# An attention and state-space kernel: another lead for the projection, another split of the products with C, and statistics that end later

## The chip, the cores and the metric

The kernel runs on one core of a Trainium2 chip. The metric is the device time of one execution in microseconds (us), from the first instruction to the last. In what follows PE is TensorE (the matmuls), PEld its weight loads, DVE is VectorE, ACT is ScalarE, POOL is GpSimd, and SP is SyncE, which here only issues DMAs. Each of these takes its instructions strictly in the order of the program, and an instruction that waits for a semaphore holds all that stand behind it on its engine.

## The reference, cut to what matters

The input is two images of 256 x 256 positions with 128 channels. Layer 0 is an attention along one image axis, added to its input. Layer 1, the part that matters here, is a state-space block, again added to its input:

```python
g = group_norm(x)                         # 32 groups of 4 channels, over a whole image
xi, z = split(g @ in_proj_w.T)            # 256 inner channels each
xi = silu(depthwise_conv3x3(xi) + conv_b)
dts, Bs, Cs = split(x_proj_w @ xi)        # 8, 16 and 16 rows
delta = softplus(dt_w @ dts + dt_b)
# for each of 256 channels and 16 states, along all 65536 positions of an image:
h[t] = exp(delta[t] * A) * h[t - 1] + (delta[t] * xi[t]) * B[t]
y[t] = sum over states of h[t] * C[t] + D * xi[t]
y = layer_norm(y) * silu(z)
x = x + y @ out_proj_w.T
```

## The kernel before, in words

**Stages.** After the weights are prepared, the statistics of the first image are taken, and the attention of both images runs (L289 to L568). It writes its result x1 to DRAM, and gathers the statistics of x1 on the side. `group_stats` (L204) turns them into a scale `rs` and a shift `sh` for each channel: 32 aggregations on DVE, a matmul with a matrix of 1/128 that averages over partitions, six small operations on DVE, two more matmuls, a power on GpSimd and a last operation on DVE. This happens once for each image and layer; the last of the four ends just ahead of the scan stage.

**Strips, units, slots.** The scan stage works on strips of 4 image rows (T = 1024 positions), 64 for each image, 128 in all. A strip has NU = 32 units: two halves `h` of the channels, in each four groups `m` of states, in each four quarters `q` of 32 channels. A unit is 128 partitions (32 channels x 4 states) x 1024 positions. The order of the stage is written out by hand in the loop at L1051: slot t is the turn of unit t, and the emitted order is the order on PE, ACT, DVE and GpSimd. Below, a slot of the strip is t modulo 32.

In slot t, in this order: `fetch(t + 6)` issues the loads for a later unit; on odd t `drive(t + 3)` (L960) multiplies `du` by B for the pair of units t + 3 and t + 4 on GpSimd, in one instruction of 128 x 2048; `products(t - 2)` (L994) multiplies both units of a *pooled* pair by C on GpSimd; `decay(t + 1)` (L952) is the exponential on ACT, which goes to one of two tiles `da` in PSUM; `scan(t)` (L973) is the recurrence on DVE, 128 x 1024; `product(t)` (L985) multiplies by C on DVE, if the unit is not pooled; `y_out` (L1034) copies the finished y of half the channels out of PSUM on ACT, once every 16 slots; then come pieces of other work that are due in this slot; then `start_up` and `add_up` (L1007, L1017), matmuls that start y with D x and sum products over states; last `remember(t)` (L980), which keeps the last state of the unit on ACT.

A pooled unit's scan writes into `hb`, in SBUF, which GpSimd can read; the others write over `da`. Before, the pairs that begin at units 6, 14, 22, 26 and 30 are pooled, so DVE has 22 of the 32 products of a strip. I number pairs by 0 to 15: drive 13 works for units 26 and 27. The three buffers of `hb` hold a pair each, the three of `du_r` two quarters each.

**Other work in the slots.** `project(k)` (L621) makes what strip k needs, placed by `base`: normalise and transpose x1, 4 times 9 convolution matmuls, the gate z, B, C and delta; three big functions on ACT of 128 x 2048, each between two loads of function tables (`silu_z` at base + 28, `silu_xs` at base + 36, `softplus` at base + 52); and two products `times` on GpSimd (base + 55 and 56). The results are stored to DRAM tiles (`xs_d`, `sz_d`, `bc_d`, `delta_d`, `du_d`) and read back, spread over the partitions, by `fetch`: `bb` and `cc` (B and C of four units), `delta_r` and `du_r` (a quarter of 32 channels). All pieces of `project` that need a PSUM bank take turns in one bank. `finish(k)` (L805) does the layer norm, the gate and the output projection of strip k, a row every 8 slots.

`base` is `k * NU - 72` (L625): the projection of strip k starts 72 slots ahead of the strip's first scan.

**The DMA queue.** SP is not ordered by hand. The framework puts its DMAs in the order in which it estimates that they can be issued; each waits in that order for the engine that made its data or that frees its buffer. In the program of before, the store `sz_d` of strip k + 1 stands in this queue between the loads `du_r` of quarters 1 and 2 of strip k's first half, seven places ahead of the load of quarter 3.

Of the kernel before, what the change touches and what calls it, by code (L numbers as in the profile page):

```python
# [8 lines left out]
F32 = mybir.dt.float32  # L9
AF = mybir.ActivationFunctionType  # L10
ALU = mybir.AluOpType
# [4 lines left out]
P = 128  # L16
# [5 lines left out]
def attn_then_ssm_kernel(  # L22
# [46 lines left out]
    def column(name, src):  # L69

        t = const.tile([P, 1], F32, name=name)
        nc.sync.dma_start(out=t, in_=src.rearrange("(p o) -> p o", o=1))
        return t

# [5 lines left out]

    ident = const.tile([P, P], F32, name="ident")
    make_identity(nc, ident)
    ones_mean = const0.tile([P, P], F32, name="ones_mean")
    nc.vector.memset(ones_mean, 1.0 / P)
# [15 lines left out]
    bq_c = column("bq_c", bq)  # L100
    bv1_c = column("bv1_c", bv1)
# [99 lines left out]
    nc.vector.tensor_tensor(centre[:, P : 2 * P], centre[:, P : 2 * P], ident, ALU.add)  # L201


    def group_stats(stats, pool, psum, name, tag="mm"):  # L204
# [5 lines left out]
        gm_ps = psum.tile([P, G], F32, name="gm_ps", tag=tag)  # L210
        nc.tensor.matmul(gm_ps, ones_mean, mv[:, :, 0], start=True, stop=True)
        gm = pool.tile([P, G], F32, name="gm")
        nc.vector.tensor_copy(gm, gm_ps)
        dev = pool.tile([P, G], F32, name="dev")
        nc.vector.tensor_tensor(dev, mv[:, :, 0], gm, ALU.subtract)
        dev2 = pool.tile([P, G], F32, name="dev2")
        nc.vector.tensor_tensor(dev2, dev, dev, ALU.mult)
        pv = pool.tile([P, G], F32, name="pv")
        nc.vector.tensor_tensor(pv, dev2, mv[:, :, 1], ALU.add)
        ex = pool.tile([P, 2, G, CG], F32, name="ex")  # L220
        nc.vector.tensor_copy(ex[:, 0], gm.unsqueeze(2).to_broadcast([P, G, CG]))
        nc.vector.tensor_copy(ex[:, 1], pv.unsqueeze(2).to_broadcast([P, G, CG]))
        cs_ps = psum.tile([P, 2], F32, name="cs_ps", tag=tag)
        for i in range(2):
            nc.tensor.matmul(
                cs_ps[:, i : i + 1],
                ex[:, i].rearrange("p g c -> p (g c)"),
                ones_mean[:, 0:1],
                start=True,
                stop=True,  # L230
            )
        cs = pool.tile([P, 2], F32, name="cs")
        nc.vector.tensor_copy(cs, cs_ps)
        ve = pool.tile([P, 1], F32, name="ve")
        nc.vector.tensor_scalar(ve, cs[:, 1:2], GN_EPS, None, ALU.add)
        rs = const.tile([P, 1], F32, name=f"rs_{name}")
        nc.gpsimd.tensor_tensor(rs, ve, neg_half[:, 0:1], ALU.pow)
        sh = const.tile([P, 1], F32, name=f"sh_{name}")
        nc.vector.tensor_scalar(sh, cs[:, 0:1], rs, -1.0, ALU.mult, ALU.mult)
        return rs, sh  # L240

    gn0 = {}
    TT = 32
# [31 lines left out]
    NL = LG // LQ  # L275
    NA = W // LQ
    gn1 = {}
    with ExitStack() as actx:
        ap1 = actx.enter_context(tc.tile_pool(name="at1", bufs=1))
        ap = actx.enter_context(tc.tile_pool(name="at", bufs=2))  # L280
# [49 lines left out]
        def project(n, tag, name, w):  # L330
            o = calls[n]
            o[name + "_ps"] = bank(tag, f"{name}_ps", [P, TB])
            nc.tensor.matmul(o[name + "_ps"], w, o["xnc"], start=True, stop=True)
# [150 lines left out]
            nc.vector.bn_stats(stats1[b][:, gr, i, :], x1g[:, :, :, gr * CG : (gr + 1) * CG])  # L484

        def gather(to, b, stats, layer):
            to[b] = group_stats(stats, ap1, ps, f"{layer}_{b}", "t0")

        held = {}

# [96 lines left out]
    NU = NCG * NSG  # L587
    NM = NQ * NSG

    POOLED = (6, 14, 22, 26, 30)  # L590
    s1 = ctx.enter_context(tc.tile_pool(name="s1", bufs=1))
    s2 = ctx.enter_context(tc.tile_pool(name="s2", bufs=2))
    s3 = ctx.enter_context(tc.tile_pool(name="s3", bufs=3))
# [23 lines left out]
    def exp_and_ln():  # L617

        nc.scalar.preload_act_table_set("natural_log_exp_and_others")

    def project(k):  # L621

        b, s = steps[k]
        rs, sh = gn1[b]
        base = k * NU - 72  # L625
        n = min(R, H - 1 - R * s)
        v = given[k] = {}
        o = {}

        def load():  # L630

# [20 lines left out]
                nc.gpsimd.memset(xn[:, 2 + n, 1 : W + 1], 0.0)  # L652

        def turn(src, r, m):
            t_ps = o["t"] = ps_p.tile([P, RB, W], F32, name="t_ps", tag="p")
# [14 lines left out]

        def conv(h, i, taps):
            if taps[0] == 0:
                o["u"] = ps_p.tile([P, RB, W], F32, name="u_ps", tag="p")
# [24 lines left out]
            nc.sync.dma_start(out=v["xs"].rearrange("h p t -> p h t"), in_=o["xs"])  # L698

        def gate(h, i):  # L700
            o["z"] = ps_p.tile([P, RB, W], F32, name="z_ps", tag="p")
# [19 lines left out]
            nc.sync.dma_start(out=v["sz"].rearrange("h p t -> p h t"), in_=o["sz"])  # L721

        def states(i):
            o["xd_ps"] = ps_p.tile([64, TB], F32, name="xd_ps", tag="p")
# [15 lines left out]
            nc.sync.dma_start(out=v["bc"][:, cols], in_=o["xd"][32:64, cols])  # L740

        def size(h, i):
            o["dt"] = ps_p.tile([P, TB], F32, name="dt_ps", tag="p")
# [168 lines left out]
    def unit(t):  # L912

        k, i = divmod(t, NU)
        h, i = divmod(i, NM)
        m, q = divmod(i, NQ)
        return k, h, m, q
# [29 lines left out]
                )  # L947

    def pooled(t):
        return t % NU - t % 2 in POOLED  # L950

    def decay(t):  # L952
        k, h, m, q = unit(t)
# [31 lines left out]
    def product(t):  # L985
        k, h, m, q = unit(t)
        u = units[t]
        if t % 2 == 0:
            yc = s4.tile([P, 2, T], F32, name="yc")
            for i in range(2):  # L990
                units[t + i]["yc"] = yc[:, i, :]
        nc.vector.tensor_tensor(u["yc"], u["h"], repeats["cc", k, h, m], ALU.mult)  # L992

    def products(t):  # L994

        k, h, m, q = unit(t)
        hb = units[t]["pair"]
        yc = s4.tile([P, 2, T], F32, name="yc")
        for i in range(2):
            units[t + i]["yc"] = yc[:, i, :]  # L1000
        nc.gpsimd.tensor_tensor(  # L1001
            yc, hb, repeats["cc", k, h, m].unsqueeze(1).to_broadcast([P, 2, T]), ALU.mult
        )
# [114 lines left out]
```

## Time and profile before

| | us |
|---|---|
| median of 3 runs | 16278.99 (16275.81 to 16286.14) |
| the profiled execution | 16300.5 |
| its span, first to last instruction | 16298.5 |
| first scan (L978) | 2678.9 |
| start of the last scan | 16238.6 |
| DVE busy | 14642.8 |
| GpSimd busy | 13035.7 |
| ACT busy | 10842.9 |
| PE busy, mean granted clock | 13879.5, 0.935 |

In the lists of groups a line names the source line, the engine, the operation, the tiles out<-in, their shapes and the count; after the bar stand the busy time, the mean in ns, and how long the engine stood idle just before them and for whom. Rows of the timeline have the start, the time taken, the engine, the line and the tiles, and in brackets the idle time before and its cause. The cause is inferred from semaphores: where several were waited for, it is the last by the record. DMA rows on SP show the issue, not the transfer.

GpSimd's large operations are regular in this trace: a drive takes 4492 to 4597 ns, a pooled pair's product 4503 to 4605, a `times` 2337 to 2401. So are DVE's: a scan 2323 to 2359, a product 1223 to 1227. The decay takes 1101 to 1146 ns on ACT.

### The profile page before, as it was taken

How to read it: one execution, taken by the hardware profiler on the slowest of the kernel's cores; microseconds unless marked ns; L12 is line 12 of the kernel's file. 1: busy time of each engine (PE TensorE's matmuls, PEld its weight loads, DVE VectorE, ACT ScalarE, POOL GpSimd, SP SyncE). 2: the span in 40 equal slices, each digit the busy share in tenths (PEclk: the TensorE clock that was granted, in tenths of full speed). 3: DMA queues.
4: the chain of work that ended last, by engine and by line, in shares of the span. 5: the costliest groups of instructions: out<-in, count | busy, mean ns of one | idle time of the engine just before them, and what ended most of it. 6: DMA issues, size and time to landing. Idle time of an engine off the chain costs nothing. (4 is left out here: it accounts for less than half of the span.)

```text
span 16298.5 us, 178168 instructions
## 1 busy us (share of the span) xinstructions
PE 13879.5 (85%) x59451; PEld 7046.9 (43%) x59451; DVE 14642.8 (90%) x12484; ACT 10842.9 (67%) x20003; POOL 13035.7 (80%) x3216
## 2 busy tenths in 40 slices
PE   6999997888888888888888888888888888888886
PEld 5877783333333333333333333333333333333333
DVE  7665555999999999999999999999999999999998
ACT  3555554667666666766666666666776676677665
POOL 0111114999999999999999999999999999999998
PEclk9999998999999999999999999999999999999998
DMA  4322223666666666666666666666666666666665
GB/s 183 132 92 78 94 78 135 236 233 237 237 230 233 237 233 236 239 232 235 232 237 232 232 229 234 236 234 234 238 234 233 234 237 233 236 239 232 234 232 180
DMA packets 1428907, 3452.13 MB, mean 212 GB/s; under 512 B 119784, under 2 KB 711184, under 8 KB 1407504
## 3 DMA queue, kind: packets, MB, share of 16 engines
q1 hardware_dynamic: 1427984, 3440.73, 61.0%
q8 instruction: 468, 7.67, 0.2%
q14 instruction: 455, 3.73, 0.1%
HBM read 2752.41 MB, written 687.88 MB: 211 GB/s over the span
## 5 line engine op out<-in xcount | busy, mean ns | idle before, releaser
L966 POOL TENSOR_TENSOR hb<-du_r,bb 128x2048 f32<-128x2048 f32 x2048 | 9237.6, 4538 | 354.3 <-DVE da L978 296.2
L978 DVE TENSOR_TENSOR_SCAN da<-da,state,hb 128x1024 f32<-128x1024 f32 x2816 | 6607.2, 2346 | 163.1 <-ACT da L956 160.2
L676 PE MATMUL u_ps<-xn,w_tap 128*128 128x512 f32 x9216 | 4481.8, 629 | 617.0 <-ACT state L983 607.5
L956 ACT ACTIVATE da<-delta_r,a_neg 128x1024 f32<-128x1024 f32 x4096 | 4588.5, 1120 | 91.8 <-ACT state L983 0.4
L992 DVE TENSOR_TENSOR yc<-da,cc 128x1024 f32<-128x1024 f32 x2816 | 3449.1, 1225 | 287.3 <-PE y L1024 113.8
L1001 POOL TENSOR_TENSOR yc<-hb,cc 128x2048 f32<-128x2048 f32 x640 | 2908.7, 4545 | 527.6 <-ACT state L983 493.0
L978 DVE TENSOR_TENSOR_SCAN hb<-da,state,hb 128x1024 f32<-128x1024 f32 x1280 | 2941.9, 2336 | 199.1 <-ACT state L983 166.4
L676 PEld LDWEIGHTS u_ps<-xn,w_tap 128*128 128x128 f32 x9216 | 1762.1, 201 | 3108.4 <-issue 2110.6
L1024 PE MATMUL y<-yc,sel 128*32 128x512 f32 x16384 | 2409.3, 712 | 16.6 <-POOL yc L1001 16.6
L435 POOL TENSOR_TENSOR x1g<-xc,bo_all 128x512 f32<-128x512 f32 x256 | 315.7, 1271 | 1844.3 <-DVE stats L484 1843.1
L983 ACT COPY state<-da 128x1 f32<-128x1 f32 x2816 | 458.2, 163 | 1266.7 <-DVE yc L992 1262.4
L828 PE MATMUL yt<-centre,ys 128*128 128x256 f32 x4096 | 1029.7, 395 | 250.2 <-ACT ob L889 250.2
L1024 PEld LDWEIGHTS y<-yc,sel 128*32 128x32 f32 x16384 | 477.4, 121 | 1743.3 <-issue 1518.6
L702 PE MATMUL z_ps<-xn,w_z 128*128 128x512 f32 x1024 | 691.8, 763 | 628.2 <-ACT sz L713 389.6
L385 ACT ACTIVATE e<-s_ps,nmx 128x256 f32<-128x256 f32 x1024 | 479.4, 478 | 967.9 <-DVE nmx L376 956.7
L983 ACT COPY state<-hb 128x1 f32<-128x1 f32 x1280 | 247.0, 193 | 1262.2 <-DVE hb L978 1262.2
L828 PEld LDWEIGHTS yt<-centre,ys 128*128 128x128 f32 x4096 | 741.3, 191 | 430.1 <-ACT ob L889 347.8
L744 PE MATMUL dt_ps<-xd,w_dt 8*128 8x512 f32 x1024 | 611.7, 678 | 345.2 <-ACT state L983 193.7
L889 ACT COPY ob<-o_ps 128x256 f32<-128x256 f32 x512 | 191.0, 373 | 948.6 <-PE o_ps L879 948.0
L879 PE MATMUL o_ps<-w_out,szr 128*128 128x128 f32 x4096 | 799.2, 277 | 0.0
L879 PE MATMUL o_ps<-w_out,yg 128*128 128x128 f32 x4096 | 797.9, 277 | 0.0
L352 DVE TENSOR_TENSOR v<-v_ps,bv_all 128x512 f32<-128x512 f32 x256 | 177.1, 692 | 594.5 <-PE v_ps L345 594.5
(133 smaller groups left out, 17404.3 us busy)
## 6 DMA issues: line engine op xcount, KB each, us to landing
bb<-bc_d SPq DMA_DIRECT2D x1024, 512.0 KB, 4.2
cc<-bc_d SPq DMA_DIRECT2D x1024, 512.0 KB, 4.8
delta_r<-delta_d SPq DMA_DIRECT2D x1024, 512.0 KB, 6.6
du_r<-du_d SPq DMA_DIRECT2D x1024, 512.0 KB, 5.5
sz_d<-sz SPq DMA_DIRECT2D x128, 1024.0 KB, 6.6
szr<-sz_d SPq DMA_DIRECT2D x512, 256.0 KB, 4.1
xs_d<-xs SPq DMA_DIRECT2D x128, 1024.0 KB, 9.0
xr<-xs_d SPq DMA_DIRECT2D x256, 512.0 KB, 5.7
```

Of the source, the lines that this page charges most:

```text
L676: nc.tensor.matmul(o["u"], w_tap[:, h, tap, :], xn[:, i * RB + dy : i * RB + dy + RB, dx : dx + W], start=(tap == 0), stop=(tap == 8),)
L702: nc.tensor.matmul(o["z"], w_z[:, h, :], xn[:, 1 + i * RB : 1 + (i + 1) * RB, 1 : W + 1], start=True, stop=True,)
L744: nc.tensor.matmul(o["dt"], w_dt[:, h, :], o["xd"][0:DR, i * TB : (i + 1) * TB], start=True, stop=True,)
L828: nc.tensor.matmul(o["yt"][:, j, :], ys[k, h][:, t0 + j * P : t0 + (j + 1) * P], centre[:, (1 - h) * P : (1 - h) * P + DI], start=(h == 0) ...
L879: nc.tensor.matmul(o["o"][:, j, :], o[by][:, h, j * P : (j + 1) * P], w_out[:, i, h, :], start=False, stop=(j == WT - 1 and h == NH - 1 an ...
L956: nc.scalar.activation(da, spreads["delta", k, h, q], AF.Exp, scale=a_neg[:, g, m : m + 1])
L966: nc.gpsimd.tensor_tensor(hb, spreads["pair", k, h, q], repeats["bb", k, h, m].unsqueeze(1).to_broadcast([P, 2, T]), ALU.mult,)
L978: nc.vector.tensor_tensor_scan(u["h"], u["da"], u["hb"], st, ALU.mult, ALU.add)
L983: nc.scalar.copy(st, units[t]["h"][:, T - 1 : T])
L992: nc.vector.tensor_tensor(u["yc"], u["h"], repeats["cc", k, h, m], ALU.mult)
L1001: nc.gpsimd.tensor_tensor(yc, hb, repeats["cc", k, h, m].unsqueeze(1).to_broadcast([P, 2, T]), ALU.mult)
L1024: nc.tensor.matmul(y[q * CQ : (q + 1) * CQ, cols], sel, units[t + q]["yc"][:, cols], start=False, stop=(m == NSG - 1),)
```

## The change

Six edits, made together:

- `base` becomes `(k - 2) * NU`, 64 slots ahead of the strip's first scan in place of 72. All pieces of `project` move 8 slots later against the scan.
- The pooled pairs begin at 6, 10, 14, 22 and 30, and unit 13 is pooled alone: eleven units in place of ten have their product on GpSimd. The single's product is emitted in slot 14, ahead of scan 14, and it is half of a `yc` tile whose other half DVE writes.
- `y_out` moves from ahead of the other pieces of its slot to the slot's end, behind `remember`.
- `group_stats` is split. For the second image of layer 1 the aggregations stay at the end of the attention, and the rest becomes two pieces in slots -2 and -1, in front of the first scan. They use the PSUM bank of `finish` and a tile of it.
- The averages use a column block of the matrix `centre` (-1/256), and a factor of -2 in the copies out of PSUM, so `ones_mean` goes; some constants live only as long as the attention stage.
- In the projection of strip 0 alone, the pieces take turns in two PSUM banks, its own and that of `finish`.

The core of the diff:

```diff
+    def group_means(stats, pool):
         mv = pool.tile([P, G, 2], F32, name="mv")
         for g in range(G):
             nc.vector.bn_aggr(mv[:, g, :], stats[:, g, :, :])
...
+        return mv
+    def group_scales(mv, pool, psum, name, tag="mm", work="gw"):
...
+        def means():
+            gm_ps = psum.tile([P, G], F32, name="gm_ps", tag=tag)
+            nc.tensor.matmul(gm_ps, centre[:, 0:P], mv[:, :, 0], start=True, stop=True)
...
+        def scales():
...
+            nc.gpsimd.tensor_tensor(rs, ve, neg_half[:, 0:1], ALU.pow)
+            nc.vector.tensor_scalar(sh, cs[:, 0:1], rs, -1.0, ALU.mult, ALU.mult)
+        return (rs, sh), (means, scales)
...
         def gather(to, b, stats, layer):
-            to[b] = group_stats(stats, ap1, ps, f"{layer}_{b}", "t0")
+            if (layer, b) == (1, B - 1):
+                last.append(group_means(stats, const))
+            else:
+                to[b] = group_stats(stats, ap1, ps, f"{layer}_{b}", "t0")
...
-    POOLED = (6, 14, 22, 26, 30)
+    POOLED = (6, 10, 14, 22, 30)
+    SINGLE = 13
...
+    gn1[B - 1], pieces = group_scales(last[0], s1, ps_f, f"1_{B - 1}", "f", "yn")
+    for i, piece in enumerate(pieces):
+        at(i - 2, piece)
...
-        base = k * NU - 72
+        base = (k - 2) * NU
...
+        def bank(shape, name):
+            o["n"] = o.get("n", 0) + (k == 0)
+            pool, tag = ((ps_p, "p"), (ps_f, "f"))[o["n"] % 2]
+            return pool.tile(shape, F32, name=name, tag=tag)
...
     def pooled(t):
-        return t % NU - t % 2 in POOLED
+        return t % NU - t % 2 in POOLED or t % NU == SINGLE
...
-        nc.vector.tensor_tensor(u["yc"], u["h"], repeats["cc", k, h, m], ALU.mult)
+        eng = nc.gpsimd if pooled(t) else nc.vector
+        eng.tensor_tensor(u["yc"], u["h"], repeats["cc", k, h, m], ALU.mult)
...
             if 0 <= t - 2 < end and t % 2 == 0 and pooled(t - 2):
                 products(t - 2)
+            if 0 <= t - 1 < end and (t - 1) % NU == SINGLE:
+                product(t - 1)
...
-            if 0 <= t - 7 < end and unit(t - 7)[2:] == (NSG - 1, 0):
-                y_out(t - 7)
             others, on_pe = slots.pop(t, ((), ()))
...
             if 0 <= t < end:
                 remember(t)
+            if 0 <= t - 7 < end and unit(t - 7)[2:] == (NSG - 1, 0):
+                y_out(t - 7)
```

More of the change, by code (lines that the diff above doesn't have):

```diff
@@ L67, in attn_then_ssm_kernel, with column @@
     dram_bc = ctx.enter_context(tc.tile_pool(name="dram_bc", bufs=3, space=DRAM))
-    def column(name, src):
-        t = const.tile([P, 1], F32, name=name)
+    def column(name, src, pool=const):
+        t = pool.tile([P, 1], F32, name=name)
         nc.sync.dma_start(out=t, in_=src.rearrange("(p o) -> p o", o=1))
@@ L82, in attn_then_ssm_kernel @@
     make_identity(nc, ident)
-    ones_mean = const0.tile([P, P], F32, name="ones_mean")
-    nc.vector.memset(ones_mean, 1.0 / P)
     ln_eps = const.tile([P, 1], F32, name="ln_eps")
@@ L99, in attn_then_ssm_kernel @@
     wo = const0.tile([P, P], F32, name="wo")
-    bq_c = column("bq_c", bq)
-    bv1_c = column("bv1_c", bv1)
+    bq_c = column("bq_c", bq, const0)
+    bv1_c = column("bv1_c", bv1, const0)
     bv2_all = const0.tile([P, C], F32, name="bv2_all")
@@ L201, in attn_then_ssm_kernel @@
     nc.vector.tensor_tensor(centre[:, P : 2 * P], centre[:, P : 2 * P], ident, ALU.add)
-    def group_stats(stats, pool, psum, name, tag="mm"):
+    def group_means(stats, pool):
         mv = pool.tile([P, G, 2], F32, name="mv")
@@ L209, in group_stats @@
             nc.vector.bn_aggr(mv[:, g, :], stats[:, g, :, :])
[L210 to L240, printed above, removed]
+        return mv
@@ new lines, in group_scales @@
+    def group_scales(mv, pool, psum, name, tag="mm", work="gw"):
+        keep = const0 if name[0] == "0" else const
+        rs = keep.tile([P, 1], F32, name=f"rs_{name}")
+        sh = keep.tile([P, 1], F32, name=f"sh_{name}")
+        MEAN = -DI / P
+        o = {}
+        def means():
+            gm_ps = psum.tile([P, G], F32, name="gm_ps", tag=tag)
+            nc.tensor.matmul(gm_ps, centre[:, 0:P], mv[:, :, 0], start=True, stop=True)
+            w = o["w"] = pool.tile([P, 2, 2 * P], F32, name=work)
+            gm, dev, dev2, pv = (w[:, 1, i * G : (i + 1) * G] for i in range(4))
+            nc.vector.tensor_scalar(gm, gm_ps, MEAN, None, ALU.mult)
+            nc.vector.tensor_tensor(dev, mv[:, :, 0], gm, ALU.subtract)
+            nc.vector.tensor_tensor(dev2, dev, dev, ALU.mult)
+            nc.vector.tensor_tensor(pv, dev2, mv[:, :, 1], ALU.add)
+            ex = o["ex"] = w[:, 0, :].rearrange("p (i g c) -> p i g c", g=G, c=CG)
+            nc.vector.tensor_copy(ex[:, 0], gm.unsqueeze(2).to_broadcast([P, G, CG]))
+            nc.vector.tensor_copy(ex[:, 1], pv.unsqueeze(2).to_broadcast([P, G, CG]))
+        def scales():
+            cs_ps = psum.tile([P, 2], F32, name="cs_ps", tag=tag)
+            for i in range(2):
+                nc.tensor.matmul(
+                    cs_ps[:, i : i + 1],
+                    o["ex"][:, i].rearrange("p g c -> p (g c)"),
+                    centre[:, 0:1],
+                    start=True,
+                    stop=True,
+                )
+            cs, ve = o["w"][:, 1, P : P + 2], o["w"][:, 1, P + 2 : P + 3]
+            nc.vector.tensor_scalar(cs, cs_ps, MEAN, None, ALU.mult)
+            nc.vector.tensor_scalar(ve, cs[:, 1:2], GN_EPS, None, ALU.add)
+            nc.gpsimd.tensor_tensor(rs, ve, neg_half[:, 0:1], ALU.pow)
+            nc.vector.tensor_scalar(sh, cs[:, 0:1], rs, -1.0, ALU.mult, ALU.mult)
+        return (rs, sh), (means, scales)
@@ L242, in attn_then_ssm_kernel, with group_stats @@
+    def group_stats(stats, pool, psum, name, tag="mm"):
+        found, pieces = group_scales(group_means(stats, pool), pool, psum, name, tag)
+        for piece in pieces:
+            piece()
+        return found
     gn0 = {}
@@ L277, in attn_then_ssm_kernel @@
     gn1 = {}
+    last = []
     with ExitStack() as actx:
@@ L654, in turn @@
         def turn(src, r, m):
-            t_ps = o["t"] = ps_p.tile([P, RB, W], F32, name="t_ps", tag="p")
+            t_ps = o["t"] = bank([P, RB, W], "t_ps")
             for i in range(m):
@@ L672, in conv @@
             if taps[0] == 0:
-                o["u"] = ps_p.tile([P, RB, W], F32, name="u_ps", tag="p")
+                o["u"] = bank([P, RB, W], "u_ps")
             for tap in taps:
@@ L700, in gate @@
         def gate(h, i):
-            o["z"] = ps_p.tile([P, RB, W], F32, name="z_ps", tag="p")
+            o["z"] = bank([P, RB, W], "z_ps")
             nc.tensor.matmul(
@@ L723, in states @@
         def states(i):
-            o["xd_ps"] = ps_p.tile([64, TB], F32, name="xd_ps", tag="p")
+            o["xd_ps"] = bank([64, TB], "xd_ps")
             for h in range(NH):
@@ L742, in size @@
         def size(h, i):
-            o["dt"] = ps_p.tile([P, TB], F32, name="dt_ps", tag="p")
+            o["dt"] = bank([P, TB], "dt_ps")
             nc.tensor.matmul(
```

## The prediction, made before the run

> **What bounds the kernel now.** I read the page first: busy times, then the groups of instructions.
>
> ```profile
> PE 13879.5 (85%) x59451; PEld 7046.9 (43%) x59451; DVE 14642.8 (90%) x12484; ACT 10842.9 (67%) x20003; POOL 13035.7 (80%) x3216
> ...
> L966 POOL TENSOR_TENSOR hb<-du_r,bb 128x2048 f32<-128x2048 f32 x2048 | 9237.6, 4538 | 354.3 <-DVE da L978 296.2
> L978 DVE TENSOR_TENSOR_SCAN da<-da,state,hb 128x1024 f32<-128x1024 f32 x2816 | 6607.2, 2346 | 163.1 <-ACT da L956 160.2
> ...
> L992 DVE TENSOR_TENSOR yc<-da,cc 128x1024 f32<-128x1024 f32 x2816 | 3449.1, 1225 | 287.3 <-PE y L1024 113.8
> L1001 POOL TENSOR_TENSOR yc<-hb,cc 128x2048 f32<-128x2048 f32 x640 | 2908.7, 4545 | 527.6 <-ACT state L983 493.0
> ```
>
> The share of a whole run mixes two stages, so next come the busy times by stretch (us; PE, PEld, DVE, ACT, POOL, then clock, DMA share, GB/s):
>
> ```profile
> 4000.00:8000.00 4000.00, 3382.68 (x13598) 1523.40 (x13591) 3853.27 (x2191) 2780.30 (x4835) 3752.73 (x870) 0.93 0.69 234
> ```
>
> In the scan stage DVE is busy 96.3% and GpSimd 93.8%. PE's 85% includes waits between matmuls; its pieces run two slots late and still meet their readers. Scan starts give the step: the first of strip 1 to the first of strip 127 is 13355.5 us, 106.0 us for each of 126 strips. DVE is the bound, and GpSimd has 6.6 us to spare.
>
> The timeline of one strip (its first scan at 7973.39) shows where DVE stands still. On DVE and ScalarE:
>
> ```profile
> 8049.84 4.59 DVE L978 TENSOR_TENSOR_SCAN hb<-da,state,hb 128x1024 f32<-128x1024 f32 x2 [1.45 <-ACT state L983]
> ...
> 8064.20 2.35 DVE L978 TENSOR_TENSOR_SCAN hb<-da,state,hb 128x1024 f32<-128x1024 f32 x1 [0.22 <-ACT da L956]
> ...
> 8074.69 4.59 DVE L978 TENSOR_TENSOR_SCAN hb<-da,state,hb 128x1024 f32<-128x1024 f32 x2 [0.42 <-ACT state L983]
> ```
>
> ```profile
> 8040.44 1.01 ACT L1037 COPY ys<-y 128x1024 f32<-128x1024 f32 x1 [2.11 <-PE y L1024]
> ...
> 8045.20 1.91 ACT L718 ACTIVATE sz<-sz 128x2048 f32<-128x2048 f32 x1
> ...
> 8048.62 1.12 ACT L956 ACTIVATE da<-delta_r,a_neg 128x1024 f32<-128x1024 f32 x1
> ```
>
> The copy of y sits at the head of ScalarE's slot and waits 2.11 us for PE; everything behind it, the big SiLU and the decay of slot 22, is late. The smaller stalls lie around the pooled pair 26 and 27. GpSimd waits for DVE, never the reverse:
>
> ```profile
> 8000.12 4.54 POOL L1001 TENSOR_TENSOR yc<-hb,cc 128x2048 f32<-128x2048 f32 x1 [1.34 <-ACT state L983]
> ...
> 8020.08 4.56 POOL L966 TENSOR_TENSOR hb<-du_r,bb 128x2048 f32<-128x2048 f32 x1 [1.81 <-DVE da L978]
> ...
> 8054.66 4.55 POOL L1001 TENSOR_TENSOR yc<-hb,cc 128x2048 f32<-128x2048 f32 x1 [2.97 <-ACT state L983]
> ```
>
> **What the Trainium skill says.** "GPSIMD Engine Reference", 3.1 (elementwise accounting): a two-input fp32 operation of 2048 elements takes 4497 ns on GpSimd; here 4538. "SBUF — State Buffer", two separate sides: DVE shares a port exclusively with GpSimd where it reads two SBUF operands. Scans and products read one of two from PSUM, and the product's 1223 to 1227 ns beside a GpSimd at 94% agree that they don't share. "ScalarE: Activation LUTs", What ACT_TABLE_LOAD costs: 1283 ns and a drain of about 1380 for each switch; the trace has 1283, and SiLU starts 11 ns later, so I charge no drain. "DMA: Bandwidth & Descriptors", Anatomy of one DMA: a wait on a semaphore holds the issuing sequencer. SP, in order, agrees: its bb loads wait for GpSimd for up to 9.9 us with others behind them.
>
> **The change, part by part.**
>
> *DVE.* With each slot's shortest time over 110 strips (slot with product 3.52 to 3.60, without 2.24 to 2.27, a gating product 0.6 more in slots 5, 13, 21, 29), a strip takes 103.0; stalls make the rest, 3.0. One product fewer saves 3.52 − 2.24 = 1.28, leaving 101.75. Moving pair 26 to 10 changes no sum.
>
> *y_out behind remember.* The 1.2 to 1.6 us stall of slot 22 goes: the copy now holds only the decay after the next. Nothing else is queued behind it in its slot. What is late next is GpSimd.
>
> *GpSimd.* Start to start: drive 4.49, a pair's product 4.63 if a drive follows (else 4.49), half a pair 2.33 (2.47 before a drive). A strip: 16 × 4.49 + 4 × 4.63 + 4.49 + 2.47 + 2 × 2.32 = 102.0. That is now the busiest engine, and tied to DVE at both ends: products of units 6 and 7 follow scan 7, and drive 14 must end before scan 28. Between them lie four pairs' products, nine drives, the single and both `times`, 65.9 us (the last counted to its end). DVE from scan 28 to slot 8 of the next strip: 38.6; handing over 0.15 and 0.32. The ring closes at **105.0**. Drives 8 and 10 come late inside it: DVE then waits for `hb` at scans 16 (0.7) and 20 (1.9). Up to 3 us of ScalarE stalls hide there.
>
> *Projection 64 slots ahead.* All its pieces move 8 slots later against the scan, its DMAs too. `times` run at slots 23, 24 and feed the drive of slot 29 (before: 15, 16). More serious: the SiLU of z moves to slot 28. SP's order, as the changed program is built, is then: du_r of quarter 2, **sz_d** (waits for that SiLU), delta_r of quarter 3, **du_r of quarter 3**. Before, sz_d stood 7 places ahead, right for a SiLU of slot 20; now 2. The du_r is an input of drive 17, which GpSimd wants some 9 us after slot 28 begins. From the start of slot 28: decay at 0.31; SiLU over 4.36 later (in the strip's timeline from the decay at 8042.77 to 8047.13), so sz_d at 4.7; delta_r waits for decay 30, over at 7.3; du_r at 7.95, 0.6 behind. Its landing is the unknown: `du_r` took 3.4 to 9.2 us, median 5.5. It follows a 1 MB store and a 512 KB load. A load issued 2.6 us after the 1 MB delta_d store landed 5.9 after issue (median of 96), and loads issued together land 1.3 apart; 5.9 + 1.3 − 0.65 = 6.55. I take 6.2, as sz_d (6.6) lands faster than delta_d (7.3). Drive 17 starts at 7.95 + 6.2 + 0.1 = 14.25.
>
> Behind it on GpSimd: drive 17, products of 30 and 31, drives 18 to 21, 4.49 + 4.63 + 4 × 4.49 = 27.1, so products of 6 and 7 start at 41.3 (DVE alone: 38.9). From there to the end of drive 10, 38.8, plus 0.15; scan 20 starts at 80.3; DVE's slots 20 to 27 take 26.4. This ring closes at **106.7**, 0.7 above 106.0. With the landing at 3.4 the other ring rules, 105.0; at 7.6, 108.1.
>
> *PE, cc, bb, delta_r.* PE has the same matmuls; it waits for the products of GpSimd before add_up, and by the same sums ends the add_up that product 24 needs nearly 3 us ahead. The cc and bb behind sz_d are needed more than 6 us later. Nothing charged.
>
> *Front.* Ending the second image's statistics later takes 2541.1 to 2545.2 off the path, 4.1; two banks for the first projection spare about 11 of 17 waits of 0.67 to 0.96 between a bank's readers, 8 (bounds 3 and 12); ScalarE's first decay no longer stands behind the second strip's last SiLU. What is late then: the deferred `rs` stands behind drive 1 on GpSimd, and scan 0 behind `sh`. Drive 1 ended at 2675.1; 12 earlier is 2663, scan 0 near 2664 against 2678.85: **15** saved, from 5 to 25. Three small DVE operations with two SBUF operands may wait for a drive: below zero excluded, 4.5 each at most, within those bounds.
>
> **Sum.** The profiled execution took 16300.5 (span 16298.5): + 126 × 0.7 = 88, − 15 gives 16373. The median shown is 21.5 less: **16350**, 0.4% slower.
>
> **Rivals.** (A) The du_r lands early and the GpSimd ring of 105.0 rules: 126 × (−1.0) − 15 = −141, 16138, faster. For: du_r alone landed in 3.75. It decides from a landing below 5.4, where drive 17 starts before 13.4 and the strip falls below 106.0. Against: sz_d and delta_r are certainly in flight. This is the other side of my forecast. (B) Product and stall simply vanish: DVE 101.75 and 1 us of stalls, 126 × (−3.2) − 15, about 15860. For: DVE is the bound now. Against: GpSimd alone needs 102.0, and its ring is longer. (C) Loads pile up, since delta_r, cc and du_r of the new strip are all issued within the 12 us before: landing 7.6, 108.1, 126 × 2.1 − 15 = +250, 16529. For: loads in a burst landed in up to 9.2.
>
> **Chances.** The forecast's ring (105.9 to 107.4) 0.56, A 0.25, B 0.04, C 0.15. 0.2% is 33 us, about what a measurement of this kernel can tell from no change. Of the forecast's 0.56 some 0.13 lie within it, 0.02 below: faster 0.31, same 0.13, slower 0.56. The range 16120 to 16480 takes in A and half of C and leaves out B. The forecast's own range is 16250 to 16440.
>
> **What would show it.** Drive 17 waiting for a du_r DMA once a strip; SP waiting for the SiLU of z ahead of it; DVE waiting for GpSimd's hb at scans 16, 20, 28; GpSimd above 95%; no 1.4 us before scan 22; first scan near 2664. If GpSimd never waits for du_r, the forecast is wrong and A stands; if DVE doesn't wait for hb, B.

## The result, and the profile after

The changed kernel takes **16652.68 us** (median, 16648.71 to 16658.12) against 16278.85 before: a ratio of **1.0229, interval 1.0211 to 1.0247**, 2.3% slower. The forecast was slower by 0.4%; its range ended at 16480. The direction held and the size did not.

The profiled execution has a span of 16656.1 against 16298.5, 357.6 more. Scan starts divide that. The first scan starts at 2645.3, which is 33.6 earlier. From the first to the last scan it takes 13953.2 in place of 13559.7, 393.5 more; the step from strip to strip (the mean of 126, as in the prediction) is **109.1 us in place of 106.0**. Behind the last scan 2.3 are saved. 393.5 − 33.6 − 2.3 = 357.6: all of the loss, and more, is in the strips.

The page of the changed kernel has the same work, and other waits (L996 is now the drive, L1008 the scan, L1023 the product, L1032 the pair's product):

```profile
PE 14152.5 (85%) x59451; PEld 7124.7 (43%) x59451; DVE 14510.6 (87%) x12355; ACT 10828.6 (65%) x20003; POOL 13332.3 (80%) x3344
...
L996 POOL TENSOR_TENSOR hb<-du_r,bb 128x2048 f32<-128x2048 f32 x2048 | 9263.0, 4548 | 957.8 <-DMA du_r<-du_d 740.5
L1008 DVE TENSOR_TENSOR_SCAN da<-da,state,hb 128x1024 f32<-128x1024 f32 x2688 | 6312.3, 2348 | 861.5 <-POOL hb L996 816.1
...
L1023 DVE TENSOR_TENSOR yc<-da,cc 128x1024 f32<-128x1024 f32 x2688 | 3291.8, 1225 | 183.4 <-PE y L1055 7.3
...
L1032 POOL TENSOR_TENSOR yc<-hb,cc 128x2048 f32<-128x2048 f32 x640 | 2897.2, 4527 | 16.6 <-PE o_ps L909 11.9
...
du_r<-du_d SPq DMA_DIRECT2D x1024, 512.0 KB, 6.2
sz_d<-sz SPq DMA_DIRECT2D x128, 1024.0 KB, 9.2
```

DVE does 132 us less and its products are 128 fewer, as planned, each as long as before. But the scans wait 863 us (861.5 and 1.8, the second in a group of its own), nearly all for GpSimd's `hb`. Before they waited 362 (163.1 and 199.1), of which 133.7 are one wait ahead of the very first scan; the other 228 were nearly all for ScalarE. And GpSimd, whose waits in this stage were for DVE and ScalarE, now waits 740 us for du_r. The work shrank and the waits grew by more. PE's granted clock was lower too, 0.908 for 0.935, but DVE's products wait 7.3 us for PE in the whole run where they waited 113.8, so the loss doesn't come that way.

One strip's end, on GpSimd (the strip's scan 28 starts at 8187.84). These are drive 15 with the one ahead, then drives 16 and 17, which serve units 0 to 3 of the next strip:

```profile
8183.22 9.10 POOL L996 TENSOR_TENSOR hb<-du_r,bb 128x2048 f32<-128x2048 f32 x2
8194.94 4.57 POOL L996 TENSOR_TENSOR hb<-du_r,bb 128x2048 f32<-128x2048 f32 x1 [2.62 <-DMA du_r<-du_d]
8203.38 4.52 POOL L996 TENSOR_TENSOR hb<-du_r,bb 128x2048 f32<-128x2048 f32 x1 [3.88 <-DMA du_r<-du_d]
```

SP's queue at the same time (start, issue time, line, tiles; the row is the issue, not the transfer):

```profile
8187.24 0.51 SPq L958 DMA_DIRECT2D cc<-bc_d  x1
8187.80 0.59 SPq L972 DMA_DIRECT2D du_r<-du_d  x1
8188.58 0.51 SPq L972 DMA_DIRECT2D delta_r<-delta_d  x1
8189.18 0.55 SPq L972 DMA_DIRECT2D du_r<-du_d  x1
8191.80 0.36 SPq L751 DMA_DIRECT2D sz_d<-sz  x1
8194.42 0.51 SPq L972 DMA_DIRECT2D delta_r<-delta_d  x1
8194.99 0.75 SPq L972 DMA_DIRECT2D du_r<-du_d  x1
```

The order is the forecast one: `sz_d` stands two places ahead of the last du_r, which is issued 7.15 after scan 28 starts. It landed (its data was complete) at 8203.23, and drive 17 begins 0.15 later. Why it took 8.2 is shown by the stretch of 20 us around it (columns: length, busy PE, PEld, DVE, ACT, POOL with counts, PE clock, DMA share, GB/s):

```profile
8184.00:8204.00 20.00, 17.95 (x84) 8.77 (x76) 19.11 (x12) 14.62 (x22) 13.50 (x4) 0.92 1.02 385
```

The DMA engines are full (a share of 1.02, as a packet that starts in the stretch counts whole), at 385 GB/s. Before, the same stretch of a strip shows 0.87 and 298 GB/s:

```profile
8062.00:8082.00 20.00, 16.85 (x81) 8.04 (x82) 19.15 (x11) 17.04 (x28) 19.92 (x6) 1.00 0.87 298
```

Over 110 strips the mean of this stretch is 384 against 299 GB/s. The mean landings over the same strips, counted from the start of scan 28, show a queue that is served in order: du_r of quarter 0 at 3.6, delta_r 5.0, cc 6.3, du_r of quarter 1 7.6, delta_r 9.4, du_r of quarter 2 10.7, `sz_d` 13.3, delta_r 14.6, du_r of quarter 3 15.8. That is 1.3 to 1.8 us for each 512 KB and 2.5 for the 1 MB.

DVE pays where GpSimd comes late: scans 2 and 4, right behind drives 16 to 18, then 16, 20 and 28. These are scans 4, 20 and 28 of the strip that starts at 8091.44:

```profile
8108.51 2.36 DVE L1008 TENSOR_TENSOR_SCAN da<-da,state,hb 128x1024 f32<-128x1024 f32 x1 [1.90 <-POOL hb L996]
...
8160.71 2.36 DVE L1008 TENSOR_TENSOR_SCAN da<-da,state,hb 128x1024 f32<-128x1024 f32 x1 [1.36 <-POOL hb L996]
8187.84 2.36 DVE L1008 TENSOR_TENSOR_SCAN da<-da,state,hb 128x1024 f32<-128x1024 f32 x1 [0.63 <-POOL hb L996]
```

### The profile page after: what moved, and what is told of

Same layout as the page of the kernel before. It is cut to its first block, busy times and chain, and to the rows that moved or that the text cites. A ratio compares the mean times of both kernels' runs of the same rounds, so it can differ in the third digit from the quotient of the medians.

```text
span 16656.1 us, 178654 instructions
## 1 busy us (share of the span) xinstructions
PE 14152.5 (85%) x59451; PEld 7124.7 (43%) x59451; DVE 14510.6 (87%) x12355; ACT 10828.6 (65%) x20003; POOL 13332.3 (80%) x3344
## 5 line engine op out<-in xcount | busy, mean ns | idle before, releaser
L996 POOL TENSOR_TENSOR hb<-du_r,bb 128x2048 f32<-128x2048 f32 x2048 | 9263.0, 4548 | 957.8 <-DMA du_r<-du_d 740.5
L1008 DVE TENSOR_TENSOR_SCAN da<-da,state,hb 128x1024 f32<-128x1024 f32 x2688 | 6312.3, 2348 | 861.5 <-POOL hb L996 816.1
L706 PE MATMUL u_ps<-xn,w_tap 128*128 128x512 f32 x9216 | 4291.2, 606 | 4.3 <-ACT sz L743 3.5
L1023 DVE TENSOR_TENSOR yc<-da,cc 128x1024 f32<-128x1024 f32 x2688 | 3291.8, 1225 | 183.4 <-PE y L1055 7.3
L1008 DVE TENSOR_TENSOR_SCAN hb<-da,state,hb 128x1024 f32<-128x1024 f32 x1408 | 3231.8, 2333 | 1.8 <-ACT state L1013 1.8
L1032 POOL TENSOR_TENSOR yc<-hb,cc 128x2048 f32<-128x2048 f32 x640 | 2897.2, 4527 | 16.6 <-PE o_ps L909 11.9
L706 PEld LDWEIGHTS u_ps<-xn,w_tap 128*128 128x128 f32 x9216 | 1700.9, 194 | 2416.7 <-issue 1787.2
L1055 PE MATMUL y<-yc,sel 128*32 128x512 f32 x16384 | 2651.7, 752 | 31.1 <-POOL yc L1032 31.1
L1055 PEld LDWEIGHTS y<-yc,sel 128*32 128x32 f32 x16384 | 552.0, 127 | 1991.9 <-issue 1626.6
L732 PE MATMUL z_ps<-xn,w_z 128*128 128x512 f32 x1024 | 765.3, 838 | 744.9 <-ACT sz L743 438.9
L774 PE MATMUL dt_ps<-xd,w_dt 8*128 8x512 f32 x1024 | 720.1, 789 | 505.8 <-ACT delta L785 343.3
L909 PEld LDWEIGHTS o_ps<-w_out,yg 128*128 128x128 f32 x4096 | 669.8, 194 | 27.8
```

Source lines behind the costliest of these rows:

```text
L706: nc.tensor.matmul(o["u"], w_tap[:, h, tap, :], xn[:, i * RB + dy : i * RB + dy + RB, dx : dx + W], start=(tap == 0), stop=(tap == 8),)
L732: nc.tensor.matmul(o["z"], w_z[:, h, :], xn[:, 1 + i * RB : 1 + (i + 1) * RB, 1 : W + 1], start=True, stop=True,)
L774: nc.tensor.matmul(o["dt"], w_dt[:, h, :], o["xd"][0:DR, i * TB : (i + 1) * TB], start=True, stop=True,)
L909: nc.tensor.matmul(o["o"][:, j, :], o[by][:, h, j * P : (j + 1) * P], w_out[:, i, h, :], start=False, stop=(j == WT - 1 and h == NH - 1 an ...
L996: nc.gpsimd.tensor_tensor(hb, spreads["pair", k, h, q], repeats["bb", k, h, m].unsqueeze(1).to_broadcast([P, 2, T]), ALU.mult,)
L1008: nc.vector.tensor_tensor_scan(u["h"], u["da"], u["hb"], st, ALU.mult, ALU.add)
```

## The experiments

A ring, here as in the prediction, is a closed chain of waits from one strip to the next: at one scan DVE waits for GpSimd, at another GpSimd waits for DVE, and a strip can't be shorter than the work along the chain.

Theory L at the start: the lead of 64 makes du_r late, and that alone is the loss over the ring of 105.0. The rivals: eleven products on GpSimd cost too much at any lead (G), or a burst of loads is late without any wait on SP (P). All times below are medians; each ratio is against the kernel before in the same comparison.

| run | strip | first scan | time | ratio, interval |
|---|---|---|---|---|
| before | 106.0 | 2678.9 | 16278.85 | |
| changed | 109.1 | 2645.3 | 16652.68 | 1.0229, 1.0211 to 1.0247 |
| e1 changed, lead 72 | 108.8 | 2655.5 | 16629.63 | 1.0214, 1.0198 to 1.0229 |
| e2 before, lead 64 | 117.1 | 2667.7 | 17695.53 | 1.0868, 1.0850 to 1.0886 |
| e3 changed, `sz_d` from ScalarE's queue | 107.8 | 2647.0 | 16486.31 | 1.0124, 1.0109 to 1.0139 |
| e4 changed, 7/8 of `sz_d` later | 107.0 | 2645.0 | 16396.00 | 1.0070, 1.0055 to 1.0085 |
| e5 changed, all of `sz_d` later | 107.1 | 2642.8 | 16404.81 | 1.0076, 1.0061 to 1.0091 |
| e6 e5 and second `times` later | 110.0 | 2644.8 | 16770.21 | 1.0301, 1.0285 to 1.0316 |
| e7 before, y_out moved | 105.2 | 2677.8 | 16188.96 | 0.9942, 0.9925 to 0.9958 |
| e8 e1, `times` 3 slots later | 106.0 | 2656.1 | 16274.38 | 0.9996, 0.9987 to 1.0004 |
| e9 e6, but `sz_d` one slot later, not seven | 105.7 | 2646.2 | 16231.66 | 0.9967, 0.9954 to 0.9980 |
| e10 e8, single unit 29 | 104.5 | 2656.9 | 16090.13 | 0.9880, 0.9865 to 0.9894 |
| e11 statistics, banks, y_out only | 105.2 | 2657.8 | 16171.82 | 0.9929, 0.9913 to 0.9946 |

### e1: the lead taken back

```diff
-        base = (k - 2) * NU
+        base = k * NU - 72
```

> The changed kernel with one edit taken back: base = k * NU - 72. In it the store sz_d stands seven places ahead of the du_r of quarter 3 again, and du_r of quarters 0 and 1 are issued some eight slots earlier against the scan. Theory L (the lead: du_r of the first half of the next strip lands late, GpSimd's drives 16 and 17 wait for it and the ring through GpSimd carries it): no wait of GpSimd for du_r, the strip falls from 109.1 to the GpSimd ring of 105.0, about 16652.7 - 126 * 4.1 = 16136, a few us more if part of the earlier first scan goes. Rival G (eleven products on GpSimd are the cost, whatever the lead): the strip stays above 107 and the time above 16400. Rival B (DVE alone): 101.75 to 103, under 15900.

Measured: 16629.63, a strip of 108.8. Theory L falls as it was put, and rival G's figures are met at this point. The waits for du_r went, and the time did not come back. All of DVE's wait for GpSimd now sits at one scan, 20 (beside it DVE waits 1.3 a strip for PE, at the product of unit 12):

```profile
DVE da L1008 <- POOL hb L996: 192.1, 37, 5.5
```

GpSimd ahead of it, from the pair product of 6 and 7 (8115.59) to the drives that begin at 8154.35, of which the first is drive 10:

```profile
8115.59 4.53 POOL L1032 TENSOR_TENSOR yc<-hb,cc 128x2048 f32<-128x2048 f32 x1 [1.89 <-ACT state L1013]
8120.19 9.00 POOL L996 TENSOR_TENSOR hb<-du_r,bb 128x2048 f32<-128x2048 f32 x2
8129.16 4.54 POOL L1032 TENSOR_TENSOR yc<-hb,cc 128x2048 f32<-128x2048 f32 x1
...
8138.26 2.36 POOL L1023 TENSOR_TENSOR yc<-hb,cc 128x1024 f32<-128x1024 f32 x1
...
8145.19 2.37 POOL L803 TENSOR_TENSOR xs<-delta,xs 128x1024 f32<-128x1024 f32 x1
8147.52 4.52 POOL L1032 TENSOR_TENSOR yc<-hb,cc 128x2048 f32<-128x2048 f32 x1
8152.01 2.37 POOL L803 TENSOR_TENSOR xs<-delta,xs 128x1024 f32<-128x1024 f32 x1
8154.35 13.52 POOL L996 TENSOR_TENSOR hb<-du_r,bb 128x2048 f32<-128x2048 f32 x3
```

With a lead of 72 the two `times` (L803) lie in this stretch, where the new pair 10 and the single 13 have been added. On the mean of 110 strips: 43.3 on GpSimd from this product to the end of drive 10, and 65.5 from scan 20 back to it, 108.8. So the eleven products have a ring of their own at each lead, and to take one of the two edits back doesn't show what it cost. e8 and e10 decide on rival G.

### e2: the lead alone

The same line, changed in the kernel before.

> The kernel before with one edit alone: base = (k - 2) * NU. Ten products on GpSimd, y_out and the statistics as before. Theory L: drive 17 waits for du_r as in the changed kernel (7.95 to its issue from the start of slot 28, 8.7 to land), and DVE waits for its hb at scan 2 and scan 4; from the start of slot 28 to scan 4 it takes 7.95 + 8.7 + 0.1 + 4.5 + 4.6 + 4.5 + 0.15 = 30.5, and DVE's slots 4 to 27 took 78.8 before: strip 109.3, about 16279 + 126 * 3.3 = 16695, slower. Rival G (the products are the cost, the lead costs nothing): 106.0 for a strip, 16279 within 30.

Measured: 17695.53. Slower, as expected, but 1410 and not 416. Here the pair 26 and 27 is still pooled, and GpSimd multiplies it during slot 28:

```profile
8611.48 4.55 POOL L1001 TENSOR_TENSOR yc<-hb,cc 128x2048 f32<-128x2048 f32 x1
```

The load cc of the next strip takes the buffer that this product reads, and SP stands until it ends, at 8616.03, with all the du_r that are still to come behind:

```profile
8608.15 0.51 SPq L942 DMA_DIRECT2D delta_r<-delta_d  x1
8616.06 0.51 SPq L928 DMA_DIRECT2D cc<-bc_d  x1
...
8619.16 0.62 SPq L942 DMA_DIRECT2D du_r<-du_d  x1
```

Drive 17 waits 9.3 in the mean of the strips. In the changed kernel that cc waits for DVE's product of unit 27 instead. So it seems to be the move of the pair from 26 to 10, which my forecast costed at nothing, that makes a lead of 64 bearable. That is read from this wait; no run moves the pair alone.

### e3, e4, e5: the wait on SP, or the bytes

e3 writes `nc.scalar.dma_start` for the store. e5 takes it out of `silu_z` (e4 leaves the first 128 of its 1024 columns there, and gives the new piece the rest):

```diff
             v["sz"] = dr.tile([NH, P, T], F32, name="sz_d")
+
+        def store_z():
             nc.sync.dma_start(out=v["sz"].rearrange("h p t -> p h t"), in_=o["sz"])
...
         at(base + 28, silu_z)
+        at(base + 35, store_z)
```

> The changed kernel with the store sz_d issued from ScalarE's queue, right behind its SiLU, in place of SP's. All bytes move at much the same time; only the wait on SP goes, and du_r of quarter 3 is issued right behind that of quarter 2. Theory L with the wait on SP as its last cause: quarter 3 lands just behind quarter 2, near 12 after the start of slot 28, so drive 17 starts right behind drive 16 (3.7 earlier than now): strip 105.4, about 16652.7 - 126 * 3.7 = 16186; GpSimd still waits some 3 for du_r of quarter 1 at drive 16. Rival P (the burst of loads alone makes it late, the wait on SP not): drive 17 still waits some 3 and the strip stays at 108.5 or more, 16580 or more.

> The changed kernel with the store sz_d cut in two: an eighth of it (128 of 1024 positions) stays where it was on SP, with its wait for the SiLU of z, and the other seven eighths are stored seven slots later, behind du_r of quarter 3. The wait stays, 0.9 of the 1 MB that stood ahead goes. If the landing of 8.7 of du_r quarter 3 comes from the 1 MB store ahead of it: it lands in 5 to 6.5, the strip is 106.7 as forecast (6.2), 16350. If it comes from the loads ahead of the store (delta_r and du_r of the other quarters): it lands in about 8, strip 108.4 or more, 16560 or more.

> The changed kernel with the whole store sz_d seven slots later: its wait and its 1 MB both stand behind du_r of quarter 3. Between the run with the wait gone but the bytes beside (107.8 for a strip) and the one with the wait kept but the bytes gone (107.0), this takes both away. Theory L (wait and bytes of this store are the whole of the excess over the GpSimd ring): drive 17 follows drive 16 with under 0.5 of wait, the strip is 105.0 to 105.5, 16652.7 - 126 * 3.8 = 16174; drive 16 still waits some 3.3 for du_r of quarter 1. Rival P (the burst of loads behind the late stores delta_d and du_d is enough): drive 17 still waits 1.5 or more, strip 107, near 16396.

Measured: strips of 107.8, 107.0 and 107.1. GpSimd's waits for du_r in the 4000 us from 4000 on, in the changed kernel and in e4:

```profile
POOL hb L996 <- DMA du_r<-du_d: 221.9, 63, 5.2
POOL hb L1004 <- DMA du_r<-du_d: 145.9, 63, 5.3
```

e4 keeps the wait and moves seven eighths of the bytes behind du_r; e5 moves the wait too, and nothing more is gained. So the wait for the SiLU costs nothing by itself: delta_r of quarter 3, also ahead of that du_r, waits for the decay of unit 30 until the same moment, and du_r is issued 7.2 after scan 28 in both. What counts is the megabyte. Without it du_r of quarter 3 lands in 6.5 in place of 8.7, and the strip falls by as much, 2.1. e4's first branch held, with 16396 for 16350, and e5's rival P was right.

e3 fell between its two forecasts. In it, du_r is issued at 2.5 (both waits are behind it), yet it lands only at 14.4, for 15.8 in the changed kernel. "DMA: Bandwidth & Descriptors" of the Trainium skill, Queues, rings and completion order, says that each DMA engine takes packets from the queues in turn. The run agrees: from a second queue the store no longer stands in line, but takes its share, and du_r of quarter 2, which was ahead of it, lands in 11.3 in place of 9.3.

### e6: less in the ring, and a store too late

```diff
-        at(base + 56, times, 1)
+        at(base + 62, times, 1)
```

> As the run before, and the second of the two products times (with its store du_d) moved from slot 24 to slot 30. Two things change: 2.3 us of GpSimd's work leaves the stretch between the products of units 6 and 7 and drive 14 for the stretch in which GpSimd waits; and on SP the second du_d no longer stands ahead of the loads du_r of quarters 0 and 1. Theory R (the ring through GpSimd, 105.0, rules once the store is away): ring 105.0 - 2.3 = 102.7, DVE alone 102.3 and GpSimd alone 102.0, so strip 103 to 103.8, 16652.7 - 126 * 5.7 = 15935, and DVE's waits at scans 16, 20, 28 shrink by 1 to 2. Rival W (what rules is the wait of drive 16 for du_r of quarter 1, 3.3, on top of GpSimd's 102.0, and it stays): strip 105.3, 16174 as the run before.

Measured: 16770.21, which neither foresaw. The wait of drive 17 for du_r did go. But SP now issued `sz_d` only in slot 2 of the next strip, behind a bb that waits for GpSimd, and there is one tile `sz`:

```profile
ACT sz L743 <- DMA sz_d<-sz: 196.7, 36, 8.1
```

ScalarE waits 5.5 a strip to write the next z, the decay of unit 5 stands behind it, and DVE behind that (3.1 at scan 5, 1.5 at scan 6). The run shows a store whose late issue is as dear as a late load; it does not judge theory R.

### e7: y_out alone

```diff
-            if 0 <= t - 7 < end and unit(t - 7)[2:] == (NSG - 1, 0):
-                y_out(t - 7)
             others, on_pe = slots.pop(t, ((), ()))
...
                 remember(t)
+            if 0 <= t - 7 < end and unit(t - 7)[2:] == (NSG - 1, 0):
+                y_out(t - 7)
```

> The kernel before with one edit alone: y_out moved behind remember. The prediction's step: the stall of 1.2 to 1.6 us ahead of scan 22 goes and DVE, the bound there with GpSimd 6.6 below it, takes the gain: strip 106.0 - 1.4 = 104.6, 16285 - 126 * 1.4 = 16109. Rival: what the copy held back is late anyway (the SiLU of z behind it still delays the decay of slot 22, or the stall shows up at the pair 26 and 27): strip within 0.3 of 106.0, 16250 to 16320.

Measured: 16188.96, 0.8 a strip. Between the two. DVE's waits:

```profile
DVE yc L992 <- PE y L1024: 45.2, 38, 1.5
DVE hb L978 <- ACT state L983: 33.6, 37, 1.6
```

The second line, 63.4 in the same 4000 us before, is halved: 0.9 is left ahead of scan 22, since the SiLU still stands in slot 20. The first was 14.8: now the product of unit 28 waits 1.2 for PE. That the later copy of y holds PE up is my reading; no run took it apart.

### e8 and e10: the other ring, with a lead of 72

```diff
-        at(base + 55, times, 0)
-        at(base + 56, times, 1)
+        at(base + 58, times, 0)
+        at(base + 59, times, 1)
```

e10 has this and `SINGLE = 29` in place of 13.

> The changed kernel with the lead of 72 (which had a strip of 108.8, with DVE waiting 5.2 for GpSimd at scan 20), and the two products times moved from slots 15 and 16 to 18 and 19, behind drive 10. Theory S (with a lead of 72 the two times lie, with the products of 6, 10, 13 and 14, between scan 7 and scan 20: 43.5 us of GpSimd from the products of 6 and 7 to the end of drive 10, plus 65.2 of DVE from scan 20 to scan 7, 108.9): the wait at scan 20 falls from 5.2 to about 1 to 1.9, the next ring, to scan 28, rules: strip 105.0, 16629.6 - 126 * 3.8 = 16151. Rival G (eleven products cost what they cost at any place): strip stays above 108.

> The run with a lead of 72 and times in slots 18 and 19 (106.0 for a strip), with the single pooled unit 29 in place of 13: its product of 2.47 on GpSimd leaves the stretch between the products of 6 and 7 and drive 12 (52.5 of GpSimd, plus 53.4 of DVE from scan 24 to scan 7, 106). Theory S (that ring rules): 106.0 - 2.5 = 103.5, 16274.4 - 126 * 2.5 = 15960; DVE alone, 101.75 and the 1.7 us of waits for PE that this lead shows in slots 12 and 13, also ends at 103.5. Rival: GpSimd or a wait for du_r rules elsewhere and it stays above 105, 16150.

Measured: e8 takes 16274.38, the same as before; e10 **16090.13**, 1.2% faster than before and the fastest here. e8 fell between its two forecasts, and so did e10 (15960 and 16150). In e8 the wait at scan 20 fell from 5.2 to 0.6, as theory S says, but I had left out the ring to scan 24, next in line:

```profile
8013.74 2.36 DVE L1008 TENSOR_TENSOR_SCAN da<-da,state,hb 128x1024 f32<-128x1024 f32 x1 [0.93 <-POOL hb L996]
8027.38 2.36 DVE L1008 TENSOR_TENSOR_SCAN da<-da,state,hb 128x1024 f32<-128x1024 f32 x1 [1.35 <-POOL hb L996]
```

It is 52.5 on GpSimd and 53.3 on DVE with 0.3 of handing over, 106.0 for 106.0 measured. e10 takes 2.5 out of it, and GpSimd's drives are then ahead of DVE throughout. DVE's only waits left are for others:

```profile
DVE yc L1023 <- PE y L1055: 49.4, 38, 2.1
DVE hb L1008 <- ACT state L1013: 48.3, 77, 0.9
```

1.3 at the product of unit 12 and 1.2 ahead of scans 22 and 30: with 102.0 of work, 104.5. Against e11 below, which has the same statistics, banks and y_out but ten products, e10 is 82 faster. So the eleven products, with the single at 29 and both `times` three slots later, are a gain when no ring closes over them, and rival G falls.

### e9: the changed kernel with its loads freed

e6 with `sz_d` stored in slot 29, which keeps it ahead of that bb.

> The changed kernel with two moves: the second of the two products times, with its store du_d, from slot 24 to slot 30, and the store sz_d from slot 28 to slot 29, which in the order of SP puts it behind du_r and delta_r of quarter 3 but ahead of the next bb (in the earlier run it stood further back, and ScalarE waited for it to free the one tile sz). Theory L+B (what the change costs is the backlog of transfers ahead of du_r): du_r of quarter 3 lands 10.4 after the start of slot 28 as in the earlier run, ScalarE doesn't wait for sz_d, drive 17 starts at 11.0 behind drive 16 and the second times; 11.0 + 27.1 + 38.8 + 27.1 = 104.0 for a strip, 16652.7 - 126 * 5.1 = 16010, faster than before. Rival W (the wait for du_r is given back to another wait, as in the runs before): strip 106 or more, 16270 or more.

Measured: 16231.66, 0.3% faster than before, strip 105.7. Most of the loss is thus gone once two stores stand elsewhere in the queue. Not all: the parts without lead and products (e11) take 16171.82, so these two still cost 60 here. It isn't the 104.0 expected: drive 16 still waits 2.0 for du_r, and a wait for ScalarE is back in the ring:

```profile
7946.25 4.59 DVE L1011 TENSOR_TENSOR_SCAN hb<-da,state,hb 128x1024 f32<-128x1024 f32 x2 [1.27 <-ACT state L1016]
```

That is scan 6, 1.2 in the mean. The copy of y waits 0.8 for PE in slot 4 of this strip; behind it on ScalarE stand a decay and the SiLU of xs, and the decay of unit 6 comes late. The products of 6 and 7 follow scan 7, and GpSimd waits 1.1 for it.

### e11: the parts without a new ring

The changed kernel with a lead of 72 and the pooled pairs of before: statistics, banks and y_out are left.

> The changed kernel with the lead back at 72 and the pooled pairs back at 6, 14, 22, 26 and 30 without a single: the parts left are the statistics with the two banks, and y_out behind remember. The first scan came 23.4 earlier with the statistics and banks at a lead of 72 (2655.5 against 2678.9), and y_out alone gave 94: with nothing shared, 16283 - 94 - 23 = 16166, first scan near 2655, strip 105.2. Rival: the earlier start is lost again in the first strips, 16189.

Measured: 16171.82, for 16166 expected. 17 lie between it and e7, with a first scan 20 earlier: the early start is kept to the end.

Lead and products, with e11's parts in three of the four corners (the corner of a lead of 64 with ten products, e2, has neither y_out nor the statistics): 72 and ten 16172, 72 and eleven 16630, 64 and ten 17696, 64 and eleven 16653. With a lead of 72 the eleven products cost 458. The lead costs 1410 beside the ten products, with the pair 26 and its cc (e2 against before, which differ in nothing else), but only 23 beside the eleven.

## Why the prediction was wrong, point by point

**The bound before** was read rightly. In e7 and e11 DVE's work is the same, it stands idle less (3.6 a strip in place of 4.1), and the strip falls to 105.2.

**DVE.** The product on GpSimd saves what was said: DVE's slots without their waits for GpSimd take 102.3, for 101.75 forecast.

**y_out.** In the changed kernel no stall is left ahead of scan 22 (slot 21 takes 4.12). With a lead of 72, where the SiLU of z is still in slot 20, 0.9 stays in e7 and e11 and 0.4 in e10. So the stall seems to go wholly only because the SiLU left slot 20 as well, which the forecast didn't say; no run takes the two apart.

**GpSimd's ring.** Drives, products and their order came as summed, and scans 16, 20 and 28 wait 1.4, 1.7 and 0.6 where 0.7 and 1.9 were forecast for the first two. GpSimd is busy 93.2% of the stage and not above 95%: it waits.

**The transfer ring: the step that failed.** The sum was 14.25 to drive 17, 27.1 to the products of 6 and 7, 38.8 to the end of drive 10, 0.15, and 26.4 of DVE: 106.7. Measured, in the mean of 110 strips: 16.06, 27.13, 38.79, 0.03, 27.12: 109.13. The mechanism is the forecast one, and the mis-sized term is "Its landing is the unknown": **6.2 taken, 8.68 measured**, beyond the 7.6 of rival C as well. Rival C, given 0.15, had named the cause, that loads pile up. With 8.68 in its place the sum gives 109.2, and the forecast would have been 16665. That it comes so near is luck in part: the issue came 0.8 earlier than forecast, and 0.7 of wait at scan 28 was left out of DVE's part; the two cancel.

I had taken the landing from loads behind one store at a quiet place and added one neighbour. What mattered was how much was in the queue. When du_r of quarter 3 is issued, 7.2 after scan 28, the mean landings above leave ahead of it the rest of du_r of quarter 1, a delta_r, du_r of quarter 2, `sz_d` and another delta_r. With itself that is some 3.3 MB, 8.6 us at 385 GB/s. The records of the transfers agree: in the mean of 95 strips 3.37 MB moved between its issue and its landing. The queue is so full because everything comes at once. Du_r of quarter 0 already took 7.0 to land, and from its issue to that of quarter 3, 10.6 us, 5120 KB are issued, both counted, which at 385 GB/s takes 13.6. A lead of 64 puts the stores `delta_d` and `du_d` at slots 24 to 26, and all that reads them follows; before, du_r of quarters 0 and 1 were issued some 22 us ahead of scan 28 and had landed some 14 ahead. e4 shows the term: 2.2 less in the landing is 2.1 less in the strip. For the same reason I missed that drive 16 waits too, 3.3 for du_r of quarter 1.

**"Now 2"** places for `sz_d` was right as a fact and wrong as a cause. e4 against e5 shows that its wait costs nothing.

**The other side, rival A,** needed a landing below 5.4. In no run with a lead of 64 did that load take less than 6.5 in the mean; e9 came below 106.0 by issuing it earlier.

**Front.** 15 forecast, 33.6 measured. The attention stage ends 3.8 earlier in this profile, which the change doesn't explain (e2, which leaves that stage as it was, has 3.2 of it). The statistics give 4.0 (4.1 forecast). From the first normalise to strip 0's softplus it takes 73.9 in place of 93.1, **19.2 for the banks where 8 was taken**, above the bound of 12 (e11, with a lead of 72, has 73.4 too; no run has the banks alone): the copies of u come every 7.73 in place of 8.77, and those of z wait 0.2 to 0.5 for PE in place of 1.22. The rest, 6.6, lies between softplus and the first scan: the lead of 64 leaves eight slots of the second strip's projection behind it. In e2, the lead alone, the first scan is 11 earlier, and 5 of these lie behind softplus.

## What to carry to other kernels

When a change moves the stores that feed a burst of loads, count the bytes that have been issued and haven't landed when a load is issued, its own with them, and divide them by the rate that the profile shows when its DMA share is near 1; a landing time from a quieter place says nothing. Where two engines feed each other across iterations, sum the ring for each step at which one needs the other (here scans 20, 24 and 28), since the longest of them rules and the next is right behind. Edits that were tuned together can't be costed one by one: the lead alone cost 1410 (e2), the eleven products alone 458 (e1 against e11), and both together 481 (the changed kernel against e11).

## What the runs showed of the hardware that was not expected

At a DMA share of 1.02, 16 engines moved 385 GB/s, and transfers from one queue landed in the order of issue, about 1.3 us apart for 512 KB, some 400 GB/s. "DMA: Bandwidth & Descriptors" of the Trainium skill, Anatomy of one DMA, has a fit for a single DMA issued from GpSimd, 2.0 us and bytes over 436e3 per us, which gives an estimate of 3.2 us for 512 KB by itself. These were issued from SP; the shortest du_r in the queue of before took 3.4, and the one here 8.7. The 5.3 us between the two are time in line, not the transfer: with seven eighths of the megabyte gone from ahead of it, in e4, it took 6.5.
